# A graph layer on one core: messages and the own term by fp32 matmuls straight from x, no wide iotas, a finer row search, single blocks between the first group's ranks

## The chip, the core and the metric

The kernel runs on one core of a Trainium2 chip. A core has a matrix engine (TensorE, PE in the profile; PEld is its weight load), a vector engine (VectorE, DVE), a scalar engine (ScalarE, ACT), GpSimd (POOL) and SyncE (SP). SP, ACT and POOL issue DMA transfers; a queue is worked through in order. Each engine works through its own list of instructions in order and meets the others at semaphores. The metric is the device time of one execution in microseconds (us), lower is better; times are medians over several executions.

## The reference

There are N = 6250 nodes with 128 features in `x`, and E = 100,000 edges sorted by destination. Each edge has a source, a destination and a type, 0 or 1.

```python
m_data = X[src] @ W_data.T + b_data
m_ctrl = X[src] @ W_control.T + b_control
msg = where(edge_type == 0, m_data, m_ctrl)
agg = segment_sum(msg, dst)
h   = x + relu(agg + X @ W_self.T + b_self)
out = (h - mean(h)) / sqrt(var(h) + 1e-5)          # over the 128 features
```

Inputs and result are fp32.

## The kernel before

The nodes are padded to 49 blocks of 128. Since a message depends on the source and the type alone, the kernel first computes every node's message for both types: 98 tiles of 128 rows (`m3`, in SBUF, with a copy `table` in DRAM). fp32 values are held as three bf16 pieces that add up to them, so a tile is 128 x 384 bf16.

**Lead-in.** The messages `y` of a block are nine bf16 matmuls (L480): `split_x` (L452 to L464) cuts `x` in three pieces by two ACT casts and two DVE subtractions for each part of up to eight blocks, `three_parts` (L289) does the same for the weights, and each piece of one meets each piece of the other. A tenth matmul adds the bias (L484). `take` (L489) casts a PSUM pair of blocks to bf16 on ACT; `leave` (L495) subtracts what was taken, by a matmul with a negative identity; three takes give the three pieces. `store` (L504) writes them to `table` on SP. `store_x` (L466) writes the pieces of `x` to DRAM (`x3_t`) for later. TensorE holds four block pairs of `y` in PSUM.

Meanwhile the edges of each block have to be found. `r0` takes the first destination of each of 125 rows of 800 edges (L232), DVE compares them with the blocks' bounds (L274), a matmul counts, and POOL fetches for each block the row in which it begins (`er`, L283). Counting in that row (L357) gives each block's first edge, a small matmul turns the column into a row (L363), and SP loads a window of 18 x 128 edges for each block from there (L380), reading the address from `first`. POOL makes index tables by iota (L243 to L253); those named `counted` are 128 x 128 x n wide with n = 5, 6 and 13.

**Groups.** 40 blocks are worked in eight groups of five (`GROUPS`). For a group, DVE computes fields of its edges (`edge_fields`, L522), a one-hot over the 98 source tiles (`hot_st`, L568), and then 18 steps give each edge a slot within its source tile (`ranks`, L572): a matmul set `tri`, a DVE maximum (L585), a matmul set `rest`, each waiting for the one before. From the slots, DVE builds `two` (L601, L606), and TensorE collects (L623) for each block, source tile and slot the row in that tile and the destination row: `vs`. These are stored (`packed`), spread over all partitions (`rows`, L737), and compared (L744).

**Sums.** For each of the 40 blocks and every four source tiles, TensorE gathers message rows by a one-hot matmul into PSUM (`g_ps`, L771), ACT evicts them as bf16 (L780), and TensorE adds them to their destinations (`agg`, through `by_columns`, L225 to L228, which issues a matmul as four of 32 columns). The own term `X @ W_self.T` joins the same PSUM sum (`own_of`, L805): three sets of four matmuls with 384 columns, the pieces of `x` from `x3_t` (`load_own`, L796) against all three pieces of the weight. The other nine blocks go another way: POOL gathers each edge's message row from `table` (`msg`, L866), 162 tiles in all, three buffers deep. Finishing is a reduction over the three pieces, the residual, statistics and an ACT pass (L186).

**The order** of all this on each engine is fixed when the program is built. `Order` (L60) plans it: each stream of work yields steps with costs in us, needs, and a lag; of the steps that can start first on an engine it takes the one with the earliest due time. `due` (L396) holds those times: `BUILT` is when sums begin, `BLOCK` the time for a block, `PACE` that for a gathered tile, `AHEAD` how long before its first use a group is to be ready. These are the author's estimates, and only the order comes of them.

Behind the sums stands a second way (`sums_over_all`), run only if the number of edges matched isn't E; with these inputs it isn't run.

Of the kernel before, what the change touches and what calls it, by code (L numbers as in the profile page):

```python
# [19 lines left out]
P = 128  # L20
# [10 lines left out]
ER = E // EC  # L31
EPS = 1e-05
# [72 lines left out]
def kernel(  # L105
# [33 lines left out]
    x3_t = dram.tile([NB, D, 3 * P], BF16, name="x3_t")  # L139
# [62 lines left out]
    with ExitStack() as main:  # L202
        sums_over_windows(main, tc, x, xt, edges, w, bias, table, x3_t, packed, total,
                          add_parts, finish, load_rows, norm)
# [6 lines left out]
def sums_over_windows(ctx, tc, x, xt, edges, w, bias, table, x3_t, packed, total,  # L211
# [19 lines left out]
    r0 = const.tile([EC, 1], I32, name="r0")  # L231
    nc.sync.dma_start(r0, edges.rearrange("(p k) c -> p (k c)", p=EC)[:, 1:2])  # L232
# [3 lines left out]
    w_sb = build.tile([D, D3], F32, name="w_sb", bufs=1)  # L236
    A.dma_start(w_sb, w)
    b1 = build.tile([1, D3], F32, name="b1", bufs=1)
    A.dma_start(b1, bias)

# [9 lines left out]
    counted = {}  # L250
    for n in sorted({DC, CH, *GROUPS}):
        counted[n] = const.tile([P, P, n], BF16, name=f"count{n}")
        G.iota(counted[n], pattern=[[1, P], [0, n]], base=0, channel_multiplier=0,  # L253
               allow_small_or_imprecise_dtypes=True)
    bound_p = const.tile([NB, 1], F32, name="bound_p")
    V.tensor_scalar_mul(bound_p, pid[:NB], float(P))
    bound_f = const.tile([EC, NB], F32, name="bound_f")
    V.tensor_scalar_mul(bound_f, iota_f[:EC, :NB], float(P))
    pid1 = const.tile([P, 1], F32, name="pid1")
    V.tensor_scalar_add(pid1, pid, 1.0)  # L260
    slot_f = const.tile([P, R], F32, name="slot_f")
    V.tensor_scalar_add(slot_f, iota_f[:, :R], SLOT)
    ones = const.tile([P, P], F32, name="ones")
    V.memset(ones, 1.0)
    ones_b = const.tile([P, P], BF16, name="ones_b")
    V.memset(ones_b, 1.0)
    ident = const.tile([P, P], F32, name="ident")
    V.tensor_scalar(ident, iota_f[:, :P], pid, None, op0=ALU.is_equal)

    r0f = work.tile([EC, 1], F32, name="r0f")
    V.tensor_copy(r0f, r0)
    begun = work.tile([EC, NB], F32, name="begun")
    V.tensor_scalar(begun, bound_f, r0f, None, op0=ALU.is_gt)  # L274
    row_ps = ps_a.tile([P, 512], F32, name="small")
    T.matmul(row_ps[:NB, 0:1], begun, ones[:EC, 0:1], start=True, stop=True)
# [4 lines left out]

# [32 lines left out]
    def constants():  # L314
# [6 lines left out]
        for i in range(3):  # L321
            A.copy(bias3[32 * i : 32 * i + 1, :], parts[0:1, i, : 2 * D])
# [734 lines left out]
```

## Time and profile before

| | |
|---|---|
| time, median of 3 runs | 694.81 us (692.65 to 695.08) |
| profiled execution, device time | 689.8 us |
| its span, first to last instruction | 688.1 us |
| TensorE's granted clock, mean | 0.979 |
| TensorE, DVE, ACT, POOL busy | 615.4, 490.4, 478.5, 213.8 us |
| first matmul of the sums, last of a group's sums | 122.1 and 673.0 us |

A line of the timeline has the start in us, the time in us, the engine (with q: its queue, where it issues a transfer), the line of the kernel, the operation, what it writes and reads, the shapes and the count; neighbours of one kind are joined. In brackets stands the idle time of the engine before it and what ended it. A line of the stretches has the stretch, its length and the busy time (and count) of PE, PEld, DVE, ACT and POOL, then the granted clock, the DMA engines' busy share and GB/s. The ends of matmuls are modelled, and they overlap, so their starts tell more than their durations.

### The profile page before, as it was taken

To read this page: it belongs to the slowest core of one execution; us is meant where nothing else is said; L and a number is where in the kernel's file an instruction comes from. 1 tells how busy PE (TensorE), PEld (TensorE's weight loads), DVE (VectorE), ACT (ScalarE), POOL (GpSimd) and SP (SyncE) were. 2 spreads that over 40 slices of the span, in tenths; PEclk is the share of its full clock that TensorE was granted. 3 is DMA by queue.
4 is the path that set the end of the run, shared out by engine and by line. 5 is a ranking of instruction groups with operands and counts; after the bars stand their busy time and mean duration, and the time that the engine had idled before them with its cause. 6 is when DMAs were issued, how large, how long until landed. Compare 5 with 4: busy or idle time off the path is not lost.

```text
span 688.1 us, 29925 instructions
## 1 busy us (share of the span) xinstructions
PE 615.4 (89%) x12874; PEld 527.2 (77%) x12874; DVE 490.4 (71%) x1021; ACT 478.5 (70%) x1140; POOL 213.8 (31%) x181
## 2 busy tenths in 40 slices
PE   1897997899989998899999989999999899998991
PEld 0675774689878887888798877888898778878880
DVE  8684456776787768866887687758975875467863
ACT  2464553677778777787787777887878677767763
POOL 6000000433354333343444342224242433242220
PEclk9999998899999999999999999999999999999996
DMA  2478745441335124432543153325421542144211
GB/s 81 125 213 236 231 141 172 159 150 49 120 104 168 55 66 160 116 99 52 187 116 103 47 182 107 102 62 182 122 88 51 185 116 90 45 161 129 78 31 50
DMA packets 63612, 81.41 MB, mean 118 GB/s; under 512 B 14356, under 2 KB 54815, under 8 KB 63423
## 3 DMA queue, kind: packets, MB, share of 16 engines
q1 hardware_dynamic: 54158, 59.41, 27.1%
q0 software_dynamic: 8160, 16.60, 9.0%
q10 hardware_dynamic: 1154, 3.41, 1.6%
q8 instruction: 102, 1.67, 1.0%
q14 instruction: 38, 0.31, 0.2%
HBM read 61.50 MB, written 17.90 MB: 115 GB/s over the span
## 4 chain that ended last, share of the span: by engine, by line
PE 77%; DMA 7%; DVE 5%; ACT 5%; issue 2%; SPq 1%; ACTq 0%; another core or an unknown queue 0%
PE agg L228 26%; PE g_ps L771 23%; PE acc L228 8%; PE small L623 7%; PE y L480 6%; PE agg_g L228 5%; ACT gs L780 4%; DMA rows<-packed 3%; DMA msg<-table,idx 3%; PE y L500 1%; DVE slot L585 1%; ACT h_p L186 1%; PE y L484 1%; DMA packed<-vs 1%; DMA win<-in_edges 0%
## 5 line engine op out<-in xcount | busy, mean ns | idle before, releaser
L780 ACT CAST gs<-g_ps 128x384 bf16<-128x384 f32 x963 | 397.6, 498 | 128.8 <-PE g_ps L771 86.9
L771 PE MATMUL g_ps<-m,rows 128*32 128x384 bf16 x4000 | 353.6, 331 | 14.1 <-ACT gs L780 8.2
L228 PE MATMUL agg<-gs,hot_d 128*32 128x384 bf16 x4000 | 346.1, 333 | 13.0 <-ACT gs L780 9.5
L866 POOL DMA_INDIRECT msg<-table,idx x162 | 188.4, 1163 | 321.6 <-PE agg_g L228 154.4
L228 PEld LDWEIGHTS <-hot_d 128*32 128x32 bf16 x4000 | 212.2, 137 | 40.9 <-issue 28.9
L771 PEld LDWEIGHTS <-rows 128*32 128x32 bf16 x4000 | 197.7, 136 | 35.3 <-issue 24.4
L585 DVE TENSOR_REDUCE slot<-acc 128x5 bf16<-128x490 f32 x144 | 95.4, 662 | 87.3 <-PE acc L228 56.5
L758 DVE TENSOR_TENSOR hot_d<-count,to 128x1664 bf16<-128x1664 bf16 x80 | 85.0, 1068 | 6.2 <-ACT to L656 4.3
L228 PE MATMUL agg_g<-msg,hot_g 128*32 128x384 bf16 x648 | 68.5, 330 | 5.3 <-DMA msg<-table,idx 5.0
L228 PE MATMUL acc<-hot_st,rest 128*32 128x490 bf16 x544 | 61.2, 377 | 9.0 <-DVE slot L585 8.4
L493 ACT CAST m<-y 128x512 bf16<-128x512 f32 (+1 forms) x75 | 40.7, 580 | 36.2 <-PE y L484 27.3
L228 PE MATMUL acc<-hot_st,tri 128*32 128x490 bf16 x576 | 64.4, 374 | 0.0
L480 PE MATMUL y<-w,x 128*128 128x256 bf16 x441 | 58.4, 289 | 3.6 <-DVE x L464 1.1
L568 DVE TENSOR_TENSOR hot_st<-count,st_b 128x2940 bf16<-128x2940 bf16 x24 | 47.7, 1992 | 12.9 <-PE small L623 11.6
L713 POOL DMA_INDIRECT msg_s<-table,row_i x8 | 14.1, 1760 | 136.8 <-DVE counts L723 109.8
L623 PE MATMUL small<-hot_st,two 128*32 128x98 bf16 x1440 | 55.5, 293 | 0.3 <-DVE two L606 0.3
L480 PEld LDWEIGHTS <-x 128*128 128x128 bf16 x441 | 45.4, 104 | 12.5 <-DVE x L464 1.8
L623 PEld LDWEIGHTS <-two 128*32 128x32 bf16 x1440 | 50.7, 119 | 1.9 <-DVE two L606 0.9
L744 DVE TENSOR_SCALAR rows<-rows,pid 128x3136 bf16<-128x3136 bf16 x40 | 41.6, 1045 | 10.2 <-DMA rows<-packed 10.2
L149 DVE TENSOR_REDUCE whole<-agg 128x128 f32<-128x384 f32 x40 | 22.1, 554 | 28.6 <-PE g_ps L771 16.0
L228 PEld LDWEIGHTS <-hot_g 128*32 128x32 bf16 x648 | 32.1, 124 | 7.9 <-issue 6.3
L228 PEld LDWEIGHTS <-rest 128*32 128x32 bf16 x544 | 23.4, 97 | 19.0 <-issue 17.0
(149 smaller groups left out, 475.9 us busy)
## 6 DMA issues: line engine op xcount, KB each, us to landing
rows<-packed SPq DMA_DIRECT2D x40, 784.0 KB
table<-m SPq DMA_DIRECT2D x10, 768.0 KB
x_p<-x_t SPq DMA_DIRECT2D x40, 96.0 KB
x_t<-x SPq DMA_DIRECT2D x5, 768.0 KB
msg<-table,idx POOLq DMA_INDIRECT x162
xt<-in_xt ACTq DMA_DIRECT2D x5, 512.0 KB
xs_p<-in_x SPq DMA_DIRECT2D x40, 64.0 KB
out<-h_p SPq DMA_DIRECT2D x8, 320.0 KB
```

The lines of the kernel that those rows point to most:

```text
L149: nc.vector.tensor_reduce(whole, agg.rearrange("p (i c) -> p c i", i=3), axis=AX.X, op=ALU.add)
L228: T.matmul(out[c : c + 32], lhsT[:, c : c + 32], rhs, **flags)
L480: T.matmul(y[:, j, :], x3s[g][:, b + j - at_part[g], i, :], w3[:, k, : 2 * D], start=i == j == k == 0, stop=False, skip_group_check=True)
L493: A.copy(part_of(b, n, i), ys[b][:, :n, :].rearrange("p b (t c) -> p t b c", t=2))
L568: V.tensor_tensor(hot, counted[n][:, None, 1 : NT + 1, :].to_broadcast([P, KC, NT, n]), fields[grp][2][:, c * KC : c * KC + KC, None, :].t ...
L585: V.tensor_reduce(slots[grp][:, k, :], by_q, axis=AX.X, op=ALU.max)
L623: T.matmul(vt[c0 : c0 + R, q // 2, :], two[:, k, i, :, q], hot[:, k, :, q], start=c == k == 0 and q < 2, stop=c * KC + k == KT - 1, skip_g ...
L744: V.tensor_scalar(rows[b], rows[b], pid1, None, op0=ALU.is_equal)
L758: V.tensor_tensor(hot, counted[DC][:, :, :n], places[grp][:, q, None, c * DC : c * DC + n].to_broadcast([P, P, n]), op=ALU.is_equal)
L771: T.matmul(g_ps[t * R : (t + 1) * R, :D3], rows[b][:, :, s], m3[:, s, :], start=True, stop=True)
L780: (A.copy if e == "A" else V.tensor_copy)(gs, g_tiles.pop((b, g))[:, :D3])
L866: G.indirect_dma_start(out=msgs[j, k], out_offset=None, in_=table[:, :], in_offset=bass.IndirectOffsetOnAxis(ap=idx[:, j, k : k + 1], axis=0),
```

## The change

Messages: `split_x`, `store_x`, `three_parts` and the bf16 pieces of the weights go. A block's `y` is one fp32 matmul from `xt` with `w_sb`, and the bias matmul. A block is a step of its own, where a pair was.

Start: the index tables `counted` are copied by ACT from a narrow iota; the bias is split first, ahead of the row search; `x` is asked for after the bias copies in ACT's order. The row search takes 500 rows of 200 edges (four entries for each partition, counted by four matmuls). The constants that DVE writes are steps with due times of their own.

Own term: one fp32 set of four matmuls of 128 columns, with a column block of `x` transposed loaded from the input (64 KB where it was 96 KB).

Order: `BUILT`, `BLOCK`, `PACE`, `AHEAD`, `LEAD` and several due times are set anew; the first group's lead is `FIRST` and its ranks get a span of 34; `v` is one step for each of the 18 columns; the indices of gathered blocks are no longer needed before `built`.

What follows in the built program's order: on SP the store of the first part of `table` stands ahead of the first window (before, seven windows stood ahead of it). On TensorE the matmul that turns `first` comes after six message blocks. In the first group's ranks mostly one message block stands between two steps. The last gathered tile is summed within block 38 of 40 (before: after block 40).

```diff
+RJ = 4
+ES = ER // RJ
...
-    r0 = const.tile([EC, 1], I32, name="r0")
-    nc.sync.dma_start(r0, edges.rearrange("(p k) c -> p (k c)", p=EC)[:, 1:2])
+    r0 = const.tile([EC, RJ], I32, name="r0")
+    nc.sync.dma_start(r0[:, :, None], edges.rearrange("(p j k) c -> p j (k c)", p=EC, j=RJ)[:, :, 1:2])
...
-        G.iota(counted[n], pattern=[[1, P], [0, n]], base=0, channel_multiplier=0,
-               allow_small_or_imprecise_dtypes=True)
...
+    for i in range(3):
+        A.copy(bias3[32 * i : 32 * i + 1, :], parts[0:1, i, : 2 * D])
...
+    V.tensor_tensor(begun, bound_f[:, None, :].to_broadcast([EC, RJ, NB]),
+                    r0f[:, :, None].to_broadcast([EC, RJ, NB]), op=ALU.is_gt)
...
+    for j in range(RJ):
+        T.matmul(row_ps[:NB, 0:1], begun[:, j, :], ones_b[:EC, 0:1], start=j == 0, stop=j == RJ - 1)
...
-    er = build.tile([NB, ER, 3], I32, name="er", bufs=1)
+    er = build.tile([NB, ES, 3], I32, name="er", bufs=1)
...
-    w3 = const.tile([D, 3, D3], BF16, name="w3")
-    left = build.tile([D, D3], F32, name="left", bufs=1)
-    three_parts([w3[:, i, :] for i in range(3)], w_sb, left)
-    order.free["V"] = 7.3
+    order.free.update(V=7.0, T=6.5, G=8.0)
...
     def constants():
...
+        for n in sorted(counted, key=lambda n: (n != GROUPS[0], n)):
+            yield step(("counts", n), {"A": 0.3 + 0.105 * n})
+            A.copy(counted[n], iota_f[:, :P, None].to_broadcast([P, P, n]))
...
-    LEAD, BUILT = 12.0, 85
-    BLOCK = 13.2
-    PACE = 3.2
-    AHEAD = 12.0
+    LEAD, BUILT = 8.0, 80
+    BLOCK = 12.6
+    PACE = 2.9
+    AHEAD, FIRST = 18.0, 14
...
-    def split_x():
...
-    def store_x():
...
     def multiply():
         for i, (g, b, n) in enumerate(two_blocks):
-            free = [("yl", two_blocks[i - YB][1])] if i >= YB else ["bias"]
-            yield step(("y", b), {"T": 1.08 * n}, ("x3", g), *free)
-            ys[b] = y = ps_y.tile([P, 2, 2 * D], F32, name="y")
             for j in range(n):
-                for i in range(3):
-                    for k in range(3):
-                        T.matmul(y[:, j, :], x3s[g][:, b + j - at_part[g], i, :],
-                                 w3[:, k, : 2 * D], start=i == j == k == 0, stop=False,
-                                 skip_group_check=True)
-            for j in range(n):
+                free = [("yl", two_blocks[i - YB][1])] if i >= YB and j == 0 else []
+                yield step(("y", b + j), {"T": 0.97}, ("xt", g), *free)
+                if j == 0:
+                    y = ys[b] = ps_y.tile([P, 2, 2 * D], F32, name="y")
+                T.matmul(y[:, j, :], xts[g][:, b + j - at_part[g], :], w_sb[:, : 2 * D],
+                         start=j == 0, stop=False, skip_group_check=True)
                 T.matmul(y[:, j, :], ones_b, bias3, start=False, stop=True, skip_group_check=True)
...
-            x3b[b] = own_pool.tile([D, 3, P], BF16, name=f"x3_{name}", bufs=bufs)
-            nc.sync.dma_start(x3b[b].rearrange("p i c -> p (i c)"), x3_t[b])
+            x_ts[b] = own_pool.tile([D, P], F32, name=f"xt_{name}", bufs=bufs)
+            nc.sync.dma_start(x_ts[b], xt[:, b * P : (b + 1) * P])
...
-            for i in range(3):
-                by_columns(aggs[b].rearrange("p (i c) -> p i c", i=3), x3b[b][:, i, :],
-                           w3[:, :, 2 * D :], start=False, stop=False, skip_group_check=True)
+            by_columns(aggs[b][:, :D], x_ts.pop(b), w_sb[:, 2 * D :], start=False, stop=False,
+                       skip_group_check=True)
...
-            free = [("gm", *gathered[i - MB])] if i >= MB else [*stored, "built", "idx"]
+            free = [("gm", *gathered[i - MB])] if i >= MB else [*stored, "idx"]
```

## The prediction

> **What bounds the kernel now.** First the page's head and its chain of work: the end is set by TensorE for 77% of the span, and no other engine has more than 5% of it.
>
> ```profile
> span 688.1 us, 29925 instructions
> PE 615.4 (89%) x12874; PEld 527.2 (77%) x12874; DVE 490.4 (71%) x1021; ACT 478.5 (70%) x1140; POOL 213.8 (31%) x181
> PE 77%; DMA 7%; DVE 5%; ACT 5%; issue 2%; SPq 1%; ACTq 0%; another core or an unknown queue 0%
> ```
>
> Shares over the span hide that there are stages, so I next asked for busy times in stretches that I cut at the first block's sums (122.1 us) and the last (673.0 us). The columns are the stretch, its length, and busy time of PE, PEld, DVE, ACT and POOL.
>
> ```profile
> 12.40:27.10 14.70, 9.12 (x51) 5.52 (x51) 13.27 (x36) 7.38 (x12) 1.14 (x1) 1.00 0.44 128
> 27.10:112.10 85.00, 80.35 (x883) 61.27 (x881) 46.91 (x75) 45.01 (x79) 0.00 (x0) 0.96 0.62 186
> 112.10:122.10 10.00, 3.55 (x43) 1.39 (x42) 8.19 (x25) 1.35 (x4) 0.00 (x0) 0.73 0.77 266
> 122.10:673.00 550.90, 521.18 (x11888) 458.28 (x11892) 406.56 (x852) 418.87 (x1033) 201.50 (x169) 1.00 0.35 108
> 673.00:688.10 15.10, 0.83 (x18) 0.40 (x10) 5.26 (x24) 4.03 (x11) 0.95 (x1) 0.62 0.18 50
> ```
>
> So 122.1 us pass before any block is summed, 551 us in the sums, 15 us after. In the lead-in TensorE is idle for most of the first 17 us, then busy 80 of 85 us with messages and the first group's ranks, then waits for two transfers. The timeline of the lead-in says why it starts late and what its order is:
>
> ```profile
> 1.77 9.13 POOL L253 IOTA count<- 128x640 bf16 x3
> 2.30 8.70 DVE L268 TENSOR_SCALAR ident<-iota_f,pid 128x128 f32<-128x128 f32 x1
> 12.40 1.15 POOL L283 DMA_INDIRECT er<-in_edges,row_i  x1 [1.50 <-DVE w L291]
> ...
> 24.78 0.34 DVE L343 COPY msg_b<-parts 1x384 bf16<-1x384 bf16 x1
> 25.15 1.28 DVE L357 TENSOR_SCALAR_CACHE_REDUCE less<-er,bound_p 49x800 bf16<-49x800 int32 x1
> 28.59 5.92 SPq L380 DMA_DIRECT2D win<-in_edges  x7
> 34.55 0.31 DVE L535 TENSOR_TENSOR rel_b<-win,base 128x90 bf16<-128x90 int32 x1 [3.14 <-DMA win<-in_edges]
> 36.05 2.13 PE L480 MATMUL y<-w,x 128*128 128x256 bf16 x18
> 104.56 2.13 PE L480 MATMUL y<-w,x 128*128 128x256 bf16 x18
> 115.48 0.34 SPq L737 DMA_DIRECT2D rows<-packed  x1
> 122.13 1.50 PE L771 MATMUL g_ps<-m,rows 128*32 128x384 bf16 x16 [2.53 <-DVE rows L744]
> ```
>
> A DVE instruction of 0.3 us lasts 8.70 us, as long as POOL's wide iotas; `er` is read at 25.15 the moment DVE has finished its constants (no idle time is noted before it); the windows follow 3.4 us later. From 40.9 us on the first group's 18 ranks are spaced 3.26 us apart (44.21, 47.46, 50.72 in the timeline): 1.97 us of that are the 18 passes of a block pair. The last rank ends at 104.9, `vs` follows at 110.6, and 11.5 us of storing, spreading and comparing rows lead to 122.1.
>
> **What the Trainium skill says.** "SBUF — State Buffer", section "SBUF: two separate sides": VectorE and GpSimd share a port pair as an exclusive lock, and the loser blocks; the 8.70 us above agree. "FP8 and Floating Point Precision", section "TensorE Precision Notes": true fp32 takes 4 passes. The trace has one small case, 49 columns, issued as two matmuls that start 0.04 us apart (0.24 us for both, 0.20 for one): 0.85 ns a column for each, twice the 0.43 of a bf16 pass (256 columns every 0.109 us), so 4 passes in all. It agrees. "TensorE: Matmul & The Clock Gate", section "Weight-path perf modes": the fast weight load is not for fp32; section "LDWEIGHTS": columns over 1.2, so 107 ns for 128. No run here shows that for fp32.
>
> **The change, part by part.**
>
> *Iotas and start.* With the wide iotas gone DVE isn't held from 2 to 10.8 us. The bias reached SBUF near 3.1 us in the packet record; its four-operation split takes 1.83 us (14.64 to 16.47), so `parts` is done near 4.9; `begun`, row search and `row_i` took 1.1 us (11.08 to 12.14 with the matmul), so `er` is asked for near 6.3 instead of 12.4. `er` then took 5.3 us by its packets (to 17.7) with 9,600 B rows; with 2,400 B I take 3.5 to 4: near 10. Cost: `x` is now asked for behind ACT's three bias copies (1.26 us), at 5.5 to 6.5 instead of 1.85; with 3.3 us to land, the first message block starts near 9 (first effective pass before: 12.4, steady from 17.3). ACT makes the counts by three copies (3,072 columns at 1.0 us per 1,024, 3.1 us), before any message waits for it.
>
> *Windows.* On SP the first table store now stands ahead of all windows, and it waits for the third bf16 piece of block 3; the small matmul that turns `first` stands behind six message blocks on TensorE. So: 9 + six blocks on a clock still partly low, 6 us, = 15; `first` 16; three takes and two leaves, 2 us, 18; five windows and their landing as now, 28.59 to 34.55, 6 us: fields at 24 (before 34.5). Fields 2.4 us, three one-hots of 2.0 us each, all three ahead of the first maximum in DVE's order: first rank's maximum at 32.5 (before 41.4).
>
> *Messages.* Now nine passes and a bias row, 10 x 0.109 = 1.09 us a block. After: two fp32 instructions of 256 columns x 2 x 0.425 = 0.218 us each, and the bias. Low end 0.54. High end: neither weight load hides (2 x 0.107) and the switch to bf16 drains (0.13 us, from the small fp32 pair's second start at 26.72 to the next weight load at 26.85): 0.90. I take 0.75, 49 x 0.34 = 17 us less. The splits vanish: ACT 14 casts, about 12 us, DVE 14 subtractions, about 14 us; ACT and DVE were busy 45 and 47 of 85 us, so alone this is worth nothing, but they stand between ranks. Seven stores of 4.8 MB leave the lead-in.
>
> *Ranks.* A step can't be shorter than tri, maximum, rest: 44.21 to 44.64, 0.67, a semaphore, 0.22: 1.43 us. With one block (0.75) and one pair of leaves (0.22) between, TensorE needs 0.43 + 0.97 = 1.40. So 18 x 1.43 = 26 us, plus what DVE does between maxima beyond the 0.76 us it has free: next fields 1.8, gathered indices with their windows 2.2, two of the `two` groups 3.2, two one-hots 2.6: 9.8. Ranks end at 68. The same tail as now (5.7 us) gives 74; some ten message blocks beyond one per step lie ahead of the last `two` in TensorE's order, about 5 us net: `vs` at 79 (now 110.6). Storing, spreading, comparing: 11.5 as now. First sums at 90.5 instead of 122.1: **31.6 us**.
>
> *Own term.* Three sets of four 384-column matmuls (0.164 us a set, 0.49) become one fp32 set of 128 columns: 0.21 if the four column groups run together as bf16 does, plus a drain, 0.32. 49 x 0.17 = 8.3 us of TensorE; the evictions on ACT (963, 76% of the stage) run close behind, so I pass on 60%: 5. Bounds 0 and 9.6. Loads shrink from 96 to 64 KB, already hidden: nothing.
>
> *Due times.* Groups are prepared 6 us earlier (AHEAD 18): the chain has 3% in `rows<-packed`; I take 2 us, bounds -4 and 6. The gathered blocks are paced at 2.9 instead of 3.2 and in the built order end with block 38. Now the last gathered tile arrives at 676.07, after block 39's sums at 673.0, and its output is issued at 681.4 against 678.2 for the last group. That leaves 15.1 - 3.5 = 11.6 us of tail: 3.5 us.
>
> Sum against the profiled execution: 90.5 + (550.9 - 7) + 11.6 = 646 us of span, 42 less than 688.1. That execution took 689.8, 1.7 over its span, and stands 5.0 under the median of 694.81: 694.8 - 42 = **652**.
>
> **Rivals.**
>
> *fp32 dear, or windows late (chance 0.22).* At 0.90 us a block TensorE, not the rank chain, sets the lead-in: 32 blocks after the first rank cost 5 us more, the first ones 3; and own saves nothing. Or the table store ahead of the windows goes late by 8 us, and everything behind `first` with it. First sums near 99, span 99 + 549 + 11.6 = 660, time 662 to 675. For it: SP works in order, and that store waits on five handovers. Against: fp32's 0.04 us spacing.
>
> *fp32 cheap (0.10).* Loads hidden, no drain: 0.54 a block, own 0.21: first sums 87, sums 537: span 636, time 628 to 640. Against: the rank chain of 1.43 us a step no longer shortens.
>
> *Slower (0.05).* Column groups of 32 don't overlap in fp32: no fp32 set with tiles is in the trace. Serial at 0.21 us a set each, four make 0.87 a block, 49 x 0.38 = 19 us lost, not enough; with unhidden loads and drains in each, doubled to 1.7, 49 x 1.2 = 59 us against a gain of 42 + 5 lost elsewhere: about 715. It decides from 1.4 us per block.
>
> *No change (0.02).* The end could hang on POOL's gathers, 162 in 552 us. But POOL waited 154 us of 322 on `agg_g` matmuls, so TensorE leads them.
>
> **How the numbers follow.** The likeliest case (0.61) covers 640 to 662 with 652 in it. The range 635 to 671 holds it, most of the dear case and half of the cheap one: 0.61 + 0.15 + 0.05. What this kernel's measurement can tell is about 0.5%, 3.5 us (its three runs span 2.4). Faster 0.93, same 0.02, slower 0.05.
>
> **What would show it.** Right: no DVE instruction of 8 us before 11 us; `er` issued near 6; fields near 24; ranks 1.4 to 1.8 us apart; `vs` near 79; first `g_ps` matmul 87 to 94; the last `agg_g` ahead of the last `agg`. Fp32 pair starts 0.22 us apart say cheap, 0.33 or more dear. Wrong: a steady stage over 555 us, own sets over 0.5 us, or windows issued after 24 us.

## The result and the profile after

The changed kernel takes 638.79 us, median of 4 runs (636.97 to 641.69). The kernel before, run beside it, takes 693.73 us (691.33 to 695.08). The ratio is 0.9215, 95% interval 0.9167 to 0.9264: 55 us less, where 42 were forecast. The time lies inside the range of 635 to 671, 13 us under the 652 that was named, and in the stretch of 628 to 640 that the prediction gave to its rival of cheap fp32.

The profiled execution took 641.69 us, its span 639.9. The page's head and its chain of work:

```profile
span 639.9 us, 28774 instructions
PE 581.3 (91%) x12337; PEld 490.8 (77%) x12337; DVE 465.0 (73%) x1005; ACT 467.2 (73%) x1127; POOL 195.0 (30%) x178
PE 73%; DVE 10%; DMA 5%; ACT 5%; issue 4%; SPq 1%; POOL 1%; ACTq 0%; DVEq 0%; POOLq 0%
```

TensorE has 34 us less to do and its share of the span even rises. On the chain of work DVE has gone from 5% to 10%. Five stretches again, cut at the first message, the first rank's matmul, 10 us ahead of the first sums, at the first sums and at the end of the last block's; the columns are the stretch, its length, and busy time of PE, PEld, DVE, ACT and POOL, then TensorE's clock, the DMA share and GB/s:

```profile
6.80:27.80 21.00, 18.18 (x93) 12.53 (x94) 9.50 (x33) 14.96 (x27) 0.21 (x1) 1.00 0.44 129
27.80:84.10 56.30, 50.14 (x500) 27.91 (x503) 32.25 (x53) 25.68 (x48) 0.00 (x0) 0.94 0.59 180
84.10:94.10 10.00, 4.31 (x67) 1.68 (x66) 7.80 (x24) 1.54 (x5) 0.00 (x0) 0.68 0.68 190
94.10:627.60 533.50, 508.37 (x11678) 448.38 (x11678) 407.91 (x864) 418.48 (x1036) 192.74 (x170) 0.99 0.35 110
627.60:639.90 12.30, 0.00 (x0) 0.00 (x0) 2.72 (x13) 2.24 (x6) 0.00 (x0) 0.61 0.12 33
```

First sums come at 94.1 us instead of 122.1 (28.0 less), the sums take 533.5 instead of 550.9 (17.4 less), and 12.3 us follow instead of 15.1 (2.8 less): 48.2 of span. In the sums TensorE is busy 12.8 us less (521.18 to 508.37) and idle 4.6 us less. The timeline of the lead-in, at the events that were shown of the kernel before (the lines between them are left out):

```profile
1.79 0.27 DVE L262 TENSOR_SCALAR ident<-iota_f,pid 128x128 f32<-128x128 f32 x1
...
5.79 1.22 POOL L287 DMA_INDIRECT er<-in_edges,row_i  x1 [3.98 <-DVE tri_f L317]
6.80 1.19 PE L464 MATMUL y<-w_sb,xt 128*128 128x256 f32 x2 [1.69 <-DMA xt<-in_xt]
9.26 0.47 DVE L353 TENSOR_SCALAR_CACHE_REDUCE less<-er,bound_p 49x200 bf16<-49x200 int32 x1
...
23.36 0.32 DVE L517 TENSOR_TENSOR rel_b<-win,base 128x90 bf16<-128x90 int32 x1 [9.39 <-DMA win<-in_edges]
...
74.18 0.67 DVE L567 TENSOR_REDUCE slot<-acc 128x5 bf16<-128x490 f32 x1 [0.82 <-PE acc L229]
83.22 0.32 ACT L617 CAST vs<-small 128x196 bf16<-128x196 f32 x1 [0.21 <-PE small L604]
87.79 0.34 SPq L718 DMA_DIRECT2D rows<-packed  x1
94.10 1.50 PE L752 MATMUL g_ps<-m,rows 128*32 128x384 bf16 x16 [1.92 <-DVE rows L725]
```

`ident` takes 0.27 us instead of 8.70; `er` is asked for at 5.8 instead of 12.4 and read at 9.3 instead of 25.2; the first group's fields start at 23.4 instead of 34.6. From the last rank (74.2, before 104.2) to `vs` it is 9 us, and 10.9 more to the first sums.

What an fp32 message costs can be read from its starts. First two blocks early in the lead-in, then two in a row later:

```profile
9.07 1.06 PE L464 MATMUL y<-w_sb,xt 128*128 128x256 f32 x2
...
10.14 1.06 PE L464 MATMUL y<-w_sb,xt 128*128 128x256 f32 x2
...
21.51 0.30 PEld L464 LDWEIGHTS y<-w_sb,xt 128*128 128x128 f32 x2
21.62 0.59 PE L464 MATMUL y<-w_sb,xt 128*128 128x256 f32 x2
22.05 0.27 PE L466 MATMUL y<-bias,ones_b 128*128 128x256 bf16 x1
22.16 0.60 PE L464 MATMUL y<-w_sb,xt 128*128 128x256 f32 x2
```

In the later pair one block starts 0.54 us after another (21.62 to 22.16): 0.43 for the fp32 pair (to the bias row at 22.05) and 0.11 for the bias row. The weight loads begin 0.11 us ahead, under the work before them, and nothing is lost where fp32 and bf16 meet. That is the prediction's low end, 0.54. Up to about 12.5 us everything on TensorE takes twice that, though the clock granted in this stretch reads 1.00: from 9.07 to 10.14 it is 1.07. The own term's set in the sums:

```profile
620.33 0.45 PE L229 MATMUL agg<-w_sb,xt_p 128*32 128x128 f32 x8
620.55 0.39 PE L229 MATMUL agg<-gs,hot_d 128*32 128x384 bf16 x4
```

All four column groups, 8 instructions, have passed in 0.22 us (620.33 to 620.55), against 0.49 for the three bf16 sets of the kernel before (from 664.27 to 664.76 there).

### The profile page after: what moved, and what is told of

It is laid out like the page before. It is cut to its first block, busy times and chain, and to the rows that moved or that the text cites. A ratio compares the mean times of both kernels' runs of the same rounds, so it can differ in the third digit from the quotient of the medians.

```text
span 639.9 us, 28774 instructions
## 1 busy us (share of the span) xinstructions
PE 581.3 (91%) x12337; PEld 490.8 (77%) x12337; DVE 465.0 (73%) x1005; ACT 467.2 (73%) x1127; POOL 195.0 (30%) x178
## 4 chain that ended last, share of the span: by engine, by line
PE 73%; DVE 10%; DMA 5%; ACT 5%; issue 4%; SPq 1%; POOL 1%; ACTq 0%; DVEq 0%; POOLq 0%
PE agg L229 26%; PE g_ps L752 24%; PE acc L229 8%; PE small L604 7%; PE agg_g L229 4%; ACT gs L761 3%; PE y L464 2%; DVE hot_st L550 2%; DVE slot L567 2%; DMA msg<-table,idx 2%; DVE two L588 2%; DMA xt<-in_xt 1%; PE y L482 1%; DMA rows<-packed 1%; DVE hr L583 1%
## 5 line engine op out<-in xcount | busy, mean ns | idle before, releaser
L752 PE MATMUL g_ps<-m,rows 128*32 128x384 bf16 x4000 | 370.3, 331 | 5.9 <-issue 2.2
L229 PE MATMUL agg<-gs,hot_d 128*32 128x384 bf16 x4000 | 359.6, 335 | 15.9 <-ACT gs L761 12.3
L229 PEld LDWEIGHTS <-hot_d 128*32 128x32 bf16 x4000 | 225.0, 137 | 43.3 <-issue 33.0
L752 PEld LDWEIGHTS <-rows 128*32 128x32 bf16 x4000 | 211.4, 137 | 24.3 <-issue 14.7
L604 PE MATMUL small<-hot_st,two 128*32 128x98 bf16 x1440 | 80.5, 291 | 1.4 <-issue 0.7
L229 PE MATMUL acc<-hot_st,tri 128*32 128x490 bf16 x576 | 68.6, 383 | 3.0 <-DVE hot_st L550 2.7
L604 PEld LDWEIGHTS <-two 128*32 128x32 bf16 x1440 | 64.8, 117 | 7.1 <-issue 3.1
L229 PEld LDWEIGHTS <-rest 128*32 128x32 bf16 x544 | 24.5, 97 | 20.0 <-issue 18.7
L694 POOL DMA_INDIRECT msg_s<-table,row_i x8 | 7.5, 942 | 104.2 <-DVE most L701 89.8
L464 PE MATMUL y<-w_sb,xt 128*128 128x256 f32 x98 | 35.1, 448 | 1.7 <-DMA xt<-in_xt 1.7
L150 DVE TENSOR_REDUCE whole<-agg 128x128 f32<-128x384 f32 x40 | 22.2, 554 | 17.4 <-PE g_ps L752 11.5
L229 PEld LDWEIGHTS <-tri 128*32 128x32 bf16 x576 | 25.0, 100 | 5.8 <-issue 5.4
```

The lines of the kernel that those rows point to most:

```text
L150: nc.vector.tensor_reduce(whole, agg.rearrange("p (i c) -> p c i", i=3), axis=AX.X, op=ALU.add)
L229: T.matmul(out[c : c + 32], lhsT[:, c : c + 32], rhs, **flags)
L464: T.matmul(y[:, j, :], xts[g][:, b + j - at_part[g], :], w_sb[:, : 2 * D], start=j == 0, stop=False, skip_group_check=True)
L604: T.matmul(vt[c0 : c0 + R, q // 2, :], two[:, k % KC, i, :, q], hot[:, k % KC, :, q], start=k == 0 and q < 2, stop=k == KT - 1, skip_group ...
L752: T.matmul(g_ps[t * R : (t + 1) * R, :D3], rows[b][:, :, s], m3[:, s, :], start=True, stop=True)
```

## Experiments

All times of stages in the table are from the trace of one execution of each kernel, in us from the span's start. Fields is the start of the first field of an edge, first and last rank are the starts of the first group's first and eighteenth maximum; sums are from the first to the last block's sums, and the tail is what follows. The time is the median of the timed runs, the ratio that to the kernel before on the same chip.

| kernel | fields | first rank | last rank | vs | first sums | sums | tail | time | ratio (95%) |
|---|---|---|---|---|---|---|---|---|---|
| before | 34.6 | 41.4 | 104.2 | 110.6 | 122.1 | 550.9 | 15.1 | 693.73 | 1 |
| after | 23.4 | 31.5 | 74.2 | 83.2 | 94.1 | 533.5 | 12.3 | 638.79 | 0.9215 (0.9167 to 0.9264) |
| *first chip* | | | | | | | | 656.81 before | |
| own_alone | 36.1 | 42.4 | 98.0 | 104.4 | 115.9 | 510.3 | 16.5 | 643.64 | 0.9792 (0.9711 to 0.9873) |
| messages_alone | 34.7 | 42.9 | 96.5 | 101.9 | 114.6 | 514.8 | 15.1 | 646.14 | 0.9842 (0.9768 to 0.9917) |
| no_iota_alone | 27.3 | 34.0 | 97.2 | 103.6 | 114.9 | 516.2 | 15.1 | 647.77 | 0.9875 (0.9800 to 0.9950) |
| old_pace | 23.1 | 31.3 | 74.6 | 82.2 | 93.8 | 510.8 | 16.4 | 622.57 | 0.9487 (0.9417 to 0.9558) |
| *second chip* | | | | | | | | 689.92 before | |
| after_again | 22.9 | 31.0 | 74.3 | 83.4 | 94.1 | 529.0 | 12.6 | 635.48 | 0.9208 (0.9189 to 0.9226) |
| arithmetic_alone | 29.5 | 35.7 | 82.7 | 88.1 | 97.6 | 525.7 | 16.6 | 643.26 | 0.9326 (0.9309 to 0.9343) |
| pairs | 19.8 | 32.0 | 70.3 | 77.8 | 88.4 | 524.0 | 12.6 | 626.85 | 0.9081 (0.9055 to 0.9106) |
| measured_costs | 22.8 | 29.0 | 73.2 | 81.0 | 90.8 | 519.3 | 12.7 | 625.97 | 0.9076 (0.9059 to 0.9094) |
| *third chip* | | | | | | | | 688.98 before | |
| after_third | 23.0 | 31.1 | 74.3 | 83.4 | 93.7 | 526.5 | 12.8 | 636.13 | 0.9240 (0.9221 to 0.9258) |
| old_pace2 | 22.3 | 30.4 | 71.8 | 79.4 | 91.0 | 543.1 | 16.7 | 654.47 | 0.9515 (0.9485 to 0.9544) |
| pairs_measured | 22.8 | 29.1 | 72.3 | 79.2 | 89.2 | 520.6 | 12.7 | 624.06 | 0.9064 (0.9025 to 0.9103) |
| after_iota | 31.7 | 39.9 | 83.4 | 92.4 | 103.2 | 529.2 | 12.6 | 645.39 | 0.9362 (0.9344 to 0.9381) |

The first chip runs the kernel before in 656.81 us, 5% quicker than it ran elsewhere. So times are compared only on one chip, and where a stage is set against the kernel before on these chips, the kernel before's stages are those of its one trace, taken elsewhere. The intervals of the first chip are wide: own_alone gains between 8 and 19 us, messages_alone between 5 and 15, no_iota_alone between 3 and 13. The kernel after, run again as it is, keeps its ratio on the second and third chip (0.9208 and 0.9240); it has no run on the first.

### The own term alone

The kernel before with the own term in fp32 straight from `xt`; the three bf16 parts of `x` are no longer stored, and still split for the messages.

```
-            x3b[b] = own_pool.tile([D, 3, P], BF16, name=f"x3_{name}", bufs=bufs)
-            nc.sync.dma_start(x3b[b].rearrange("p i c -> p (i c)"), x3_t[b])
+            x3b[b] = own_pool.tile([D, P], F32, name=f"xt_{name}", bufs=bufs)
+            nc.sync.dma_start(x3b[b], xt[:, b * P : (b + 1) * P])
...
-            for i in range(3):
-                by_columns(aggs[b].rearrange("p (i c) -> p i c", i=3), x3b[b][:, i, :],
-                           w3[:, :, 2 * D :], start=False, stop=False, skip_group_check=True)
+            by_columns(aggs[b][:, :D], x3b.pop(b), w_sb[:, 2 * D :], start=False, stop=False,
+                       skip_group_check=True)
```

> The kernel before with the own term alone changed: one fp32 set of four matmuls from x transposed in place of three bf16 sets, and so without the stores of the pieces of x. If TensorE sets the pace of the sums, the set falls from 0.49 to 0.22 us, 49 x 0.27 = 13 us, and 11 to 16 us come off the time (about 680). If ACT's evictions set it, under 5 us come off (689 or more).

Measured: 643.64 against 656.81 us, 13.2 less, which is what the first theory said; but not all of it comes where that theory looked. The first sums come at 115.9 us, 6 us ahead of the 122.1 of the kernel before. That trace is of another chip, but the lead-in is no quicker on this one: without iotas the ranks take 63.2 us here (34.0 to 97.2), and 62.9 in the kernel before. The 6 us are about the length of one wait that is gone. Among the ranks DVE works on the windows of the gathered blocks; in the kernel before and then in this one:

```profile
57.98 0.27 DVE L853 TENSOR_SCALAR far_g<-win_g 128x162 int32<-128x162 int32 x1 [6.16 <-DMA win<-in_edges]
50.57 0.25 DVE L851 TENSOR_SCALAR far_g<-win_g 128x162 int32<-128x162 int32 x1
```

Two of the seven stores of `x` stood among these windows in SP's order, at 37.3 and 38.9 us. Without them the last gathered window is issued at 47.4 us, with them at 53.3, and DVE no longer waits 6.16 us. The prediction had put nothing down for these stores.

For the sums some 6 to 8 us are left, of the 49 x 0.27 = 13.2 that TensorE no longer has to do there: 8 if what isn't lead-in or tail (1.4 us longer) is put to them, 6 against the 516.2 us that no_iota_alone takes for the sums of the kernel before on the same chip. About half passed on; the prediction had taken 60% of a smaller set. That is argued from single traces, not shown.

### The messages alone

The kernel before with its messages multiplied in fp32; `x` and the weights are still split and the parts of `x` still stored, and every message still waits for the third part of its blocks.

```
             yield step(("y", b), {"T": 1.08 * n}, ("x3", g), *free)
...
-                for i in range(3):
-                    for k in range(3):
-                        T.matmul(y[:, j, :], x3s[g][:, b + j - at_part[g], i, :],
-                                 w3[:, k, : 2 * D], start=i == j == k == 0, stop=False,
-                                 skip_group_check=True)
+                T.matmul(y[:, j, :], xts[g][:, b + j - at_part[g], :], w_sb[:, : 2 * D],
+                         start=j == 0, stop=False, skip_group_check=True)
```

> The kernel before with the nine bf16 passes of a message block replaced by one fp32 matmul; splits of x and their stores kept, order and due times kept. If TensorE's work is what the lead-in hangs on, a block falls from 1.09 to 0.54 us, 27 us of work, and 18 to 25 us come off (about 671). If the handovers between DVE, ACT and TensorE in the rank chain hold it, under 10 us come off.

Measured: 10.7 us less, and first sums at 114.6. 49 blocks at 0.54 instead of 1.09 us are 27 us less of TensorE, and three quarters of them didn't reach the first sums. The planner is still told 1.08 us a block here. TensorE's longest wait from 12.4 to 100 us is this one; the columns are who waited for whom, us in total, times, and the longest:

```profile
PE acc L228 <- DVE slot L582: 14.3, 8, 6.7
```

From 12.4 to 110 us of the kernel before, TensorE waited 4.3 us for `slot`, once. With cheap messages it waits 14.3. The longest, 6.7, isn't due to the subtractions: DVE stands 6.55 us before the gathered windows, as in the kernel before. For the rest DVE still has the subtractions of the split between its maxima. In the groups of the same trace from 12.4 to 96 us (busy us, mean ns, and idle time before with what ended it):

```profile
L460 DVE TENSOR_TENSOR xr<-xt,x 128x1024 f32<-128x1024 f32 (+2 forms) x7 | 7.6, 1088 | 6.1 <-ACT x L457 6.0
L464 DVE TENSOR_TENSOR x<-xr,x 128x1024 bf16<-128x1024 f32 (+2 forms) x7 | 7.6, 1084 | 2.8 <-ACT x L462 2.8
```

15.2 us of work, and 8.8 us in which DVE waited with the next subtraction for ACT's cast.

### The arithmetic of the change, start and due times of before

Both edits above, and without splits of `x` and `w` and without stores of `x`; the start (wide iotas, long rows), the two-block steps and the due times are those of the kernel before. The planner is told 0.55 us a block.

```
-            yield step(("y", b), {"T": 1.08 * n}, ("x3", g), *free)
+            yield step(("y", b), {"T": 0.55 * n}, ("xt", g), *free)
...
-        load_x(), split_x(), starts(), edge_fields(), ranks(), fill_c(), fill_a(), fill_b(),
+        load_x(), starts(), edge_fields(), ranks(), fill_c(), fill_a(), fill_b(),
```

> The kernel before with both fp32 changes (messages and own term), no splits and no stores of pieces; start (wide iotas, row search, constants) and due times as before. If the parts simply add, the own term's 13 and the messages' 11 us come off, and 2 to 6 more as DVE and ACT no longer split between the ranks: 0.955 to 0.965 of the kernel before. If the start was hidden behind the splits, the late start now shows in full and under 24 us come off (0.965 or more).

Measured: 46.7 us less than before, of the 54.4 that the whole change brings on the same chip. First sums at 97.6 us: 24.5 of the 28 us of the lead-in. So the arithmetic, with what it makes needless, is most of the change.

The two edits alone sum to 24 us, on their chip and with their wide intervals; some 20 us come only when both are made and the splits go. The prediction had priced the splits at nothing alone, and said that they stand between ranks. The table doesn't bear out that the gain lies there. From first to last rank the kernel before takes 62.9 us, this one 47.0; own_alone takes 7.2 off and messages_alone 9.2, which is the whole. In the lead-in some 11 us are beyond the two: 6.8 ahead of the fields, since DVE no longer splits `w` and `x` ahead of reading `er`, and 3.2 between `vs` and the first sums. The remainder is in the sums, where no split ever ran: 25.2 us less than in the kernel before, and 5.9 and 1.4 less for the two edits alone against no_iota_alone. The planner is told 0.55 instead of 1.08 us a block in this run, and the runs below show that the order alone can move the sums by 5 us and more. So what the absence of the splits is worth isn't parted from the new order that comes with it, and it stays open.

### The start, from both sides

First the kernel before with its wide count tiles copied by ScalarE from `iota_f`, and nothing else.

```
-        G.iota(counted[n], pattern=[[1, P], [0, n]], base=0, channel_multiplier=0,
-               allow_small_or_imprecise_dtypes=True)
+        A.copy(counted[n], iota_f[:, :P, None].to_broadcast([P, P, n]))
```

> The kernel before with the wide index tables copied by ACT instead of written by POOL's iotas; nothing else. If the late start is what costs, DVE and TensorE start some 8 us earlier and 6 to 9 us come off (about 686). If the edge search waits for DVE's constants and splits anyway, under 3 us come off. ACT's three copies (3 us) stand ahead of its first split.

Then the kernel after with the wide iotas put back on GpSimd ahead of everything, and the copies left out.

```
+    counted = {}
+    for n in sorted({DC, CH, *GROUPS}):
+        counted[n] = const.tile([P, P, n], BF16, name=f"count{n}")
+        G.iota(counted[n], pattern=[[1, P], [0, n]], base=0, channel_multiplier=0,
+               allow_small_or_imprecise_dtypes=True)
...
-            yield step(("counts", n), {"A": 0.3 + 0.105 * n})
-            A.copy(counted[n], iota_f[:, :P, None].to_broadcast([P, P, n]))
+            yield step(("counts", n), {"S": 0.0})
```

> The kernel after with the wide iotas on GpSimd put back ahead of everything, and no copies of counts on ScalarE. If the start passes on whole to the end: the row search is asked for 5 to 6.5 us later (at 11 to 12.4), fields and first rank 4 to 6 us later, first sums at 98 to 100, 4 to 6 us slower than the kernel after. Rival, that the lead-in of the kernel after is set by TensorE's messages and not by the fields: the fields still come later, but first sums at 94 to 96 and under 2 us slower.

Measured: 9.0 us less in the first, 9.3 us more in the second (645.39 against 636.13). Put back, the iotas also bring back the long DVE instruction, in the timeline of this kernel:

```profile
1.76 9.13 POOL L254 IOTA count<- 128x640 bf16 x3
1.79 9.18 DVE L267 TENSOR_SCALAR ident<-iota_f,pid 128x128 f32<-128x128 f32 x1
...
14.58 1.21 POOL L292 DMA_INDIRECT er<-in_edges,row_i  x1 [3.69 <-DVE tri_f L319]
```

`er` is asked for 8.7 us later than in after_third, the first message starts 8.9 us later, the fields 8.8 us, the first sums 9.5 us, the end 9.3 us: a delay at the start passes to the end whole. The expectation had the delay at 5 to 6.5 us and its passing on right. It was short because it set out from the 12.4 us of the kernel before; here the split of the bias stands behind the long instruction and ahead of the search in DVE's order, so all of it comes 8.9 us later, and with it the bias copies and the first load of `x` on ACT.

### Single blocks or pairs between the ranks

The kernel after with two blocks in one step, as the kernel before has them.

```
-            for j in range(n):
-                free = [("yl", two_blocks[i - YB][1])] if i >= YB and j == 0 else []
-                yield step(("y", b + j), {"T": 0.97}, ("xt", g), *free)
+            free = [("yl", two_blocks[i - YB][1])] if i >= YB else []
+            yield step(("y", b), {"T": 0.97 * n}, ("xt", g), *free)
+            for j in range(n):
```

> The changed kernel with a step of two message blocks where it has one, so that pairs stand between ranks again. If single blocks matter, a rank step has 0.54 + 0.22 us more on TensorE than the 1.43 us that the chain needs leave room for, 0.4 to 0.6 us a step over some 12 steps: 4 to 8 us more than the changed kernel. If the gaps in the rank chain are DVE's other work, under 2 us.

Measured: 8.6 us less than the kernel after on the same chip (626.85 against 635.48), where a loss was expected. `vs` comes 5.6 us earlier. Two of DVE's waits from 22 to 84 us, of the kernel after on this chip and then of the pairs:

```profile
DVE slot L567 <- PE acc L229: 15.9, 13, 2.3
...
DVE hot_st L550 <- PE small L604: 5.0, 3, 2.4
```

```profile
DVE slot L567 <- PE acc L229: 15.6, 14, 1.8
...
DVE hot_st L550 <- PE small L604: 0.8, 1, 0.8
```

The maximum waits for TensorE just as long with pairs (15.6 and 15.9 us). What shrinks is the wait of `hot_st` for the matmuls of `v` that free its buffer. In the kernel after, 2.6 of its 5.0 us lie between the ranks, the rest behind the last of them; with pairs all of it lies behind.

The expectation was right about one step: with pairs, a step with two message blocks in it takes 1.94 to 2.16 us where DVE does nothing but the maximum, and one with none 1.36 to 1.47. But with pairs fewer steps have messages in them, and the fields of the second group stand ahead of the first maximum, which so comes 1.0 us later although the first fields come 3.1 us earlier. From the first maximum to the last it is then 38.2 us instead of 43.3. So the pace of the first group isn't set by the length of a typical step; what stands between the ranks in all, and what waits there, sets it. The run changes the size of the steps and with it the whole order, and doesn't part the two. And of the 10.7 us between the two profiled executions 5.0 lie in the sums, where no message is left to compute; why, it doesn't show.

### The planner told what the trace shows

The kernel after with 0.54 us for a message block, 0.22 and 0.39 for an own set, and a window's landing at 4 us. Only the order of the instructions changes.

```
-                yield step(("y", b + j), {"T": 0.97}, ("xt", g), *free)
+                yield step(("y", b + j), {"T": 0.54}, ("xt", g), *free)
...
-            yield step(("o", b), {"T": 0.45 if b < NPB else 0.62}, ("xs", b), begun(b))
+            yield step(("o", b), {"T": 0.22 if b < NPB else 0.39}, ("xs", b), begun(b))
...
-            yield step(("win", b), {"S": 0.84}, "first", *free, lag=2.0)
+            yield step(("win", b), {"S": 0.9}, "first", *free, lag=4.0)
```

> The changed kernel with the planner told what the trace of it shows: 0.54 us for a message block, 0.22 and 0.39 for the own term, 0.9 us for issuing a window and 4 us for its landing. The gathered blocks' fields then stand two ranks later in DVE's order and the first maximum ahead of the third one-hot. If the rank chain's waits set the lead-in, 3 to 7 us less than the changed kernel; if they are covered by TensorE's messages, no change (within 2 us).

Measured: 9.5 us less than the kernel after on the same chip. Of the two profiled executions, which lie 12.9 us apart, 3.3 are ahead of the first sums (90.8 against 94.1) and 9.7 in the sums. The sums of the kernel after on this chip, and the first 5.9 us of them:

```profile
94.10:623.10 529.00, 506.49 (x11678) 448.27 (x11678) 407.35 (x864) 418.63 (x1036) 195.43 (x170) 0.99 0.36 111
94.10:100.00 5.90, 5.90 (x76) 3.32 (x80) 5.76 (x12) 3.11 (x8) 2.26 (x3) 0.50 0.83 328
```

The same of this kernel, with its first 1.6 us:

```profile
90.80:610.10 519.30, 501.27 (x11658) 447.44 (x11654) 406.70 (x862) 417.74 (x1036) 191.62 (x166) 1.00 0.36 110
90.80:92.40 1.60, 1.60 (x24) 0.92 (x24) 1.33 (x2) 0.99 (x3) 1.03 (x2) 0.50 1.01 423
```

TensorE is busy 5.2 us less and idle 4.5 us less for nearly the same instructions. Its wait for `rows` (1.8 us) and that for a gathered `msg` (1.2 us) are gone from its waits. The sums of the kernel after begin while TensorE is granted half its clock, for 5.9 us; here 1.6 us are left of such a stretch. Half of the 4.3 us between them, an estimate from these two lines, is 2 of the 5.2 us. The rest isn't accounted for, and which of the told costs brings the better order wasn't tried one by one.

### Both together

> The kernel after with message steps of two blocks and with the planner told the measured costs (0.54 us a block's message, 0.22 and 0.39 an own set, windows 0.9 and 4 to land). If the two gains have different causes (the pairs': fewer handovers between ranks; the costs': the order of the sums) they mostly add: 12 to 18 us faster than the kernel after, first sums at 86 to 89, sums 517 to 522. Rival, one cause (messages crowd the path to the first group's ranks, and either edit moves them off it): 7 to 11 us faster, no better than either.

Two-block steps at 0.54 us a block and the other told costs, the two diffs above put together. Measured: 624.06, 12.1 us less than the kernel after on its chip. Its ratio of 0.9064 (0.9025 to 0.9103) can't be told from that of the told costs alone, 0.9076, or of the pairs alone, 0.9081. By the ratios the two gains don't add, which speaks for one cause, the order around the first ranks, that either edit mends. Against the kernel after beside it, though, the 12.1 us stand at the foot of the first theory's 12 to 18, with 4.5 us ahead of the first sums and 5.9 in the sums. The full sum, 8.6 and 9.5, is out, since by the intervals the gain is between 9 and 15 us; between the two theories this is not settled. Any of the three is quicker than the kernels before and after.

### Due times of the steady stage

The kernel after with the three numbers of the kernel before.

```
-    BLOCK = 12.6
-    PACE = 2.9
-    AHEAD, FIRST = 18.0, 14
+    BLOCK = 13.2
+    PACE = 3.2
+    AHEAD, FIRST = 12.0, 14
```

> The changed kernel with BLOCK 13.2, PACE 3.2 and AHEAD 12 as before; all else as changed. If the new due times give the sums their 6 to 8 us beyond the own term and the shorter tail, 5 to 9 us are added (about 645). If the sums gained from the own term alone, under 3 us are added, all in the tail.

The kernel after has no run on that chip; the two were run side by side on the third:

> The kernel after as it is, beside the three others on one chip. Both theories: ratio to the kernel before 0.915 to 0.927, first sums at 94, sums 525 to 534, tail 12 to 13.

> The kernel after with the three numbers of the steady stage (block 13.2, pace 3.2, ahead 12) of the kernel before. If the new due times pay in the tail and cost a little in the sums (as the difference between the kernel after and the one with the arithmetic alone says): first sums within 1 us of the kernel after beside it, tail 3 to 4 us longer, sums 1 to 3 us shorter, in all 0 to 3 us slower. Rival, that earlier groups also shorten the sums (the 2 us of the prediction): sums longer by 2 us or more, in all 5 us or more slower.

Measured: 654.47 against 636.13 us, 18.3 more; on the first chip the ratio to the kernel before was 0.9487, here 0.9515, inside each other's intervals. First sums are 2.7 us earlier, the tail 3.9 us longer, the sums 16.6 us longer: the rival's side, and more than it named. TensorE's waits in the sums, with the old numbers and then of the kernel after beside it:

```profile
PE g_ps L752 <- DVE rows L725: 10.2, 7, 2.2
PE agg_g L229 <- DMA msg<-table,idx: 3.1, 2, 2.0
```

```profile
PE agg_g L229 <- DMA msg<-table,idx: 1.5, 1, 1.5
PE g_ps L752 <- DVE rows L725: 1.4, 1, 1.4
```

With 12 us ahead TensorE waits seven times for `rows`, 10.2 us in all; with 18 once, 1.4 us. That is 8.8 of the 16.6 us. Gathered messages are 1.6 more, waits for ACT another 3.6 (15.5 against 11.9), and TensorE is busy 2.6 us longer (507.35 against 504.76). It is granted half its clock for 8.1 us of these sums, and for 3.3 in the kernel after; half of the difference, 2.4 us, is an estimate of what this adds. Yet with the arithmetic alone the same 12 us were enough: no wait for `rows` is among its waits in the sums, which take 525.7 us. So the new numbers mend what another part of the new order opens. From the kernel with the arithmetic alone to the kernel after, on one chip, it is only 7.8 us, although the start is worth 9 by both of its runs. In the two traces the fields come 6.6 us earlier, but 4.9 of that are given back between the last rank and the first sums (14.9 us with the arithmetic alone, 19.8 in the kernel after); the tail is 4.0 us shorter and the sums 3.3 longer. Which of the single blocks, the due times and the told cost of a block (0.97 for 0.55) costs this isn't shown.

## Why the prediction was right or wrong

**Sum.** Span by terms, forecast and measured: lead-in -31.6 and -28.0, sums -7 and -17.4, tail -3.5 and -2.8: -42 and -48.2. The other 7 us of the 13 lay around the spans: the prediction added the 5.0 us by which the profiled execution stood under the median, and the profiled execution of after stands 2.9 over its own; the 652 was rounded down by 0.8.

**Start and windows: right, with some luck.** `er` forecast at 6.3, measured 5.8; fields 24 and 23.4; first maximum 32.5 and 31.5. Within it two terms were off and met: the first table store is issued at 15.2, not at 18, since the first message starts at 6.8 and not near 9; from there to the fields it is 8.2 us, where 6 were forecast. That DVE does three one-hots ahead of the first maximum was seen in its order, and costs what was said. That the wide iotas hold DVE for as long as they run is shown by the iotas put back (9.13 and 9.18 us). It agrees with the lock that the Trainium skill states, "SBUF — State Buffer", section "SBUF: two separate sides".

**Message block: the size was off.** Taken at 0.75 between 0.54 and 0.90; it measured 0.54. The switch from fp32 to bf16 was said to drain, from 0.13 us seen ahead of one weight load at 26.7 us of the kernel before; no message block shows such a gap. The four passes that the Trainium skill states, "FP8 and Floating Point Precision", section "TensorE Precision Notes", hold: 0.43 us against 0.109 for a bf16 pass. The weight load that its page "TensorE: Matmul & The Clock Gate", section "Weight-path perf modes", excludes from the fast path lies under the matmul before it and costs nothing here. Made alone, it brought the first sums 7.5 of 27 us.

**Rank step: this step failed.** The ranks were to end at 68, after 18 steps of 1.43 us and 9.8 us of other DVE work; they end at 74.8. From the first maximum's start to the last one's end it is 43.3 us, not 35.5 (34.8 if no whole step is counted behind the last start), and the starts are 2.51 us apart in the mean, not 1.4 to 1.8. The 1.43 us is reached, and undercut (1.36 from 71.33 to 72.69), but it isn't the typical step. In the eleven of the 17 steps in which DVE does nothing but the maximum, the mean is 1.92 us: 5.4 us over in all, in which the maximum waits for TensorE with its message blocks, subtractions (`leave`) and columns of `v`. Two stretches of 3.4 us at half the clock are among the ranks (from 33.0 and 43.3). In the other six DVE's own work is no more than was forecast, but it also waits: 3.0 us for the gathered windows and 2.6 for `v`, of which the sum had nothing; these six are 3.1 us over. The timeline of after shows the first wait (other lines are left out), and two steps of the short kind:

```profile
37.39 0.38 PE L229 MATMUL acc<-hot_st,tri 128*32 128x490 bf16 x4
39.84 0.27 DVE L832 TENSOR_SCALAR far_g<-win_g 128x162 int32<-128x162 int32 x1 [3.02 <-DMA win_g<-in_edges]
41.35 0.66 DVE L567 TENSOR_REDUCE slot<-acc 128x5 bf16<-128x490 f32 x1
42.07 0.39 PE L229 MATMUL acc<-hot_st,rest 128*32 128x490 bf16 x4 [2.80 <-DVE slot L567]
...
71.33 0.66 DVE L567 TENSOR_REDUCE slot<-acc 128x5 bf16<-128x490 f32 x1
72.69 0.67 DVE L567 TENSOR_REDUCE slot<-acc 128x5 bf16<-128x490 f32 x1 [0.70 <-PE acc L229]
```

The matmul that the maximum needs ends at 37.8, and the maximum starts at 41.35: DVE stands 3.02 us before gathered windows that haven't landed, works 1.5 us on them, and TensorE waits 2.80 in turn. The kernel before could have told this. Its ranks are not 3.26 us apart all along, as the prediction read them: over the 17 steps the mean is 3.70, and the longest, 9.47 us, holds the wait of 6.16 for the same windows that stands under "The own term alone". So the short step with one block in it was the wrong lever, and the run with pairs speaks for that: with the longer step `vs` came earlier.

**From the last rank to the first sums: right.** 11 us forecast to `vs`, 9.0 measured; 11.5 to the sums, 10.9.

**Own set and the sums: the size was off.** 0.32 us taken, 0.22 measured: the four column groups do run together in fp32. 49 x 0.27 = 13.2 us, where 8.3 were put down, with 5 of them passed on. In the trace of after TensorE is busy 12.8 us less in the sums and idle 4.6 us less, 17.4 where the own term and the due times were to bring 7. Of the due times the prediction says "I take 2 us, bounds -4 and 6": too narrow. Within the new order the old numbers cost 16.6 us of the sums, while with the arithmetic alone they left the sums at 525.7 us, below the kernel after's. In four runs the order of steps moved the sums by 5 to 17 us with the work unchanged, and the prediction gave it no such term. The stores of `x`, put at nothing, were worth some 6 us of the lead-in in the run that drops them. So the total is near the forecast in part because misses of both signs met: the ranks took 8 us more, the sums 10 less.

**Tail: right** in size and cause: the last gathered tile's sum is read at 606.9 us, 20.7 ahead of the end of the last block's (before, it ends 3.5 behind it), and with the old numbers the tail is again 16.7.

**Rivals.** The cheap rival had the right prices and the right time, but not the right place: it put the first sums at 87, they came at 94.1, and its sums of 537 were 3.5 over those measured. Dear fp32 and serial column groups fell with the starts of 0.54 and 0.22 us. The late table store didn't decide: it was issued ahead of the windows, at 15.2, and the fields still came at 23.4.

## What to carry to other kernels

When matmuls are made cheaper, ask what else waits around them: made alone, cheaper messages brought the first sums a quarter of what they saved, and with all that they make needless taken out as well, the lead-in fell by 24.5 us. In a serial chain across two engines, count what the in-order engine waits for at the head of its queue, not only what it works, and look for such waits in every step of the chain, not in three of them. Where a planner writes the order, wrong costs in it (such as 0.97 us for a block that takes 0.54) were worth 9.5 us of 635 here: after a change of arithmetic, measure the new instruction and tell the planner.

## What the hardware showed that was not expected

An fp32 matmul of 256 columns takes 0.43 us, 3.9 bf16 passes of 0.109, and its weight load and its change to bf16 and back cost nothing beside it; four fp32 column groups of 128 columns pass together in 0.22 us.

The kernel before took 656.8 us on one chip and 689 to 694 elsewhere. The difference lies in the sums, not in the lead-in (62.9 us of ranks in the kernel before, 63.2 in no_iota_alone on the quick chip). For the same sums, at a granted clock that reads 1.00 in both traces, no_iota_alone takes 516.2 us there and the kernel before 550.9 elsewhere; TensorE is busy 499.6 us instead of 521.2 and idle 16.6 instead of 29.7. Why is open.
